# Layer 1 of a hybrid network: weight sums spread out, norms scaled two pairs ahead, biases split early, the second expert's sums fetched first

## The chip, the cores and the metric

The kernel runs on one core of a Trainium2 chip, in one launch. The metric is the device time of that core in microseconds (us), from a run's start to its end. Before the change, three runs took 3275.79, 3277.91 and 3279.31 us; the median is 3277.91 us. A core has five engines that matter here[...]: TensorE (PE in the profile; PEld is its loading of weights), VectorE (DVE), ScalarE (ACT), GpSimd (POOL) and SyncE (SP), which here only issues transfers.

## The reference, cut to what matters

All data is float32. Layer 0 is a convolution and attention block on images of 256 channels and 32 x 32 pixels, 8 of them; the change does not touch it. Layer 1 works on the same data as 8 sequences of 1024 tokens of width 256:

```python
t = _to_tokens(x)
t = t + _L1_attn_ref(_ln_t(t), WQ, WK, WV)          # causal softmax, one head of width 256
t = t + _L1_ffn_ref(_ln_t(t), Wr, br, W1, b1, ...)  # 8 experts, all of them, gated
# _ln_t:  (v - mean) / sqrt(var + 1e-5) over the last axis
# in _L1_ffn_ref:
feat = jnp.mean(x, axis=0)                          # over the 8 sequences
w = jax.nn.softmax(feat @ Wr + br, axis=-1)
h = relu(bn(x @ W1[e] + b1[e])); h = relu(bn(h @ W2[e] + b2[e]))
y = h @ Wo[e] + bo[e]                               # summed over e with weights w
```

Because the mean `feat` goes over all sequences, no expert's output can be weighted before all sequences have been through the attention.

## The kernel before, in words

**Order of the work.** The engines' proxies `pe`, `act`, `dve` and `pool` record every instruction at line 68 and keep them in the order in which the program issues them. That is why the profile gives line 68 for nearly everything; its groups are told apart by the names of the tiles. The order itself is made by generators. The function `together(main, side, ratio)` runs two of them: each `yield` of `main` adds its microseconds to a count, and `side` is advanced while its own count is below 0.85 of it. What is left of `side` at the end is issued in one go. The number in a `yield` is an estimate by the author, and only sets the order.

**Attention stage, batch by batch.** `causal(b)` is the main line of batch `b`: for each of eight rows of 128 queries, `scores` multiplies the row with all keys (tile `s`, in two halves `h`), takes the negated maximum on VectorE (`nm`) and the exponential on ScalarE (`pr`). `norm` then masks `pr`, sums it and takes the reciprocal on VectorE, and scales it on GpSimd. `turn`, some rows later, transposes `pr` through PSUM (`tp`) into `pT`, and `product` multiplies with the values (`po`) and adds to the tokens `t` on VectorE. The side line `beside(b)` prepares the next batch: `first_norm(b + 1)`, then `second_norm(b - 1)` (the norm ahead of the experts, `z2`, with `feat` summed on GpSimd), then `keys_values(b + 1)` (`pk`, `pv`). In the last batch the side line is `second_norm(6)`, `second_norm_half(7)` and `gate`, which makes the experts' weights `wT` for the first half of the tokens (tiles `lg`, `ge`, `pwT`).

**A norm (`layer_norm`).** Tokens are transposed in pairs of 128 (`tpt`, then a ScalarE copy to `zt`), VectorE takes statistics (`st`, `mv`), GpSimd the reciprocal root `r`. Four empty `yield 1.0` follow. Then `scaled(0)` scales the first pair on VectorE in place in `zt`; and for each pair, the next pair is scaled, the pair is transposed back (`tpz`) and copied by ScalarE. The transposes `tp`, `tpt` and `tpz` share one PSUM pool of two buffers (`ps_t`); `pk`, `pv` and `po` share another of two.

**Weight sums.** Layers of the experts are multiplied by Strassen-like schemes with seven products instead of eight (`by_seven`, `layer3`), for which `weight_sums` computes sums of blocks of the weights: for 20 weight matrices, four VectorE instructions each on 128 x 128 blocks, the third in place in the weights. Expert 0 keeps its sums in memory; for the others they are stored to DRAM (`sums_d`). `causal` calls `next(sums, None)` once per row, from batch 2 on.

**Between the stages.** The attention's pools are closed, and the experts' pool `hp` and three PSUM pools are opened; `hp` takes memory that the attention's tiles had. Then come the folding of the experts' batch norms, the splitting of the output biases `bo` into a rounded part and a rest (`bo4`, transposed through `pbo` to `boT`), and the transfers on SP: tokens of the first two pieces (`fetch(0)`, `fetch(1)`, tile `te`), the last batch's second half (`lastt`, `lastf`, in `last_norm`), and the 18 tiles of sums (`ws`), expert by expert.

**Expert stage.** It loops over 16 half batches and 8 experts. For each piece, layer 1 (`pa`), layer 2 of the piece two before (`pm`) and layer 3 of the piece four before (`q`, in four PSUM banks) are interleaved in four steps; `last_norm` advances beside the first pieces.

## Time and profile before

| | us |
|---|---|
| median of three runs | 3277.91 |
| the profiled execution: its time | 3277.43 |
| its span, first to last instruction | 3275.3 |
| TensorE busy | 3047.3 |
| VectorE busy | 2417.4 |
| ScalarE busy | 1438.2 |
| TensorE's wait for the scaling `zt`, 1415 to 2030 us | 39.9 |

Layer 0 takes the span's first 1400 us or so, the attention of layer 1 goes to about 2036 us, and the experts fill the rest, where TensorE is busy all the time (400.00 of 400 us between 2200 and 2600). A line of the order of time reads: start, duration, engine, line, operation, output and inputs, shape, count, and in brackets how long the engine sat idle before it and whose end released it. A line of the waits reads: who waited, for whom, us in total, how often, the longest. The mean granted clock of TensorE was 0.977 of full speed.

### The profile page before, as it was taken

Reading aid. Unit: us, or ns where it says so; the run is one execution under the profiler, and the core shown is the slowest. Engines: PE = TensorE matmul, PEld = TensorE weight load, DVE = VectorE, ACT = ScalarE, POOL = GpSimd, SP = SyncE. Lnnn points to the kernel's source line nnn. Section 1 sums busy time; section 2 is a strip of 40 time slices with the busy share of each in tenths; the row PEclk is TensorE's granted clock in tenths of the full one; section 3 lists DMA queues with packets and bytes.
Section 4 is the critical chain, followed back from the end, with each engine's and each line's share of the span. In section 5 each row is a group of like instructions: output and inputs, shape, how many; then the busy total and the mean of one; then the engine's idle time right before and its main releaser. Section 6 shows DMA issues by size and latency. Waiting matters only on the chain.

```text
span 3275.3 us, 43158 instructions
## 1 busy us (share of the span) xinstructions
PE 3047.3 (93%) x17218; PEld 2050.7 (63%) x17218; DVE 2417.4 (74%) x3796; ACT 1438.2 (44%) x2227; POOL 327.9 (10%) x472
## 2 busy tenths in 40 slices
PE   7997999999999997779999998899999999999999
PEld 4554555555555554346556665678787777787787
DVE  5388888888888886735555444688888878888887
ACT  4554555555555553223333322444444444444443
POOL 2110212111111100011222111000000000000000
PEclk9998999999999999889999999999999999999999
DMA  3202020202020200031111101200000100000000
GB/s 111 53 1 52 27 52 27 53 27 52 27 52 27 52 14 20 4 136 44 50 61 51 39 26 72 75 20 20 20 20 20 33 20 20 20 20 26 20 7 13
DMA packets 49831, 121.45 MB, mean 37 GB/s; under 512 B 7302, under 2 KB 20054, under 8 KB 45782
## 3 DMA queue, kind: packets, MB, share of 16 engines
q1 hardware_dynamic: 49622, 118.61, 11.6%
q8 instruction: 137, 2.24, 0.3%
q14 instruction: 72, 0.59, 0.1%
HBM read 48.20 MB, written 37.88 MB: 26 GB/s over the span
## 4 chain that ended last, share of the span: by engine, by line
PE 48%; DVE 6%; ACT 1%; issue 1%; POOL 1%; DMA 0%; SPq 0%; ACTq 0%; POOLq 0%; DVEq 0%
PE pm L68 13%; PE pa L68 12%; PE q L68 12%; PE s L68 4%; PE po L68 3%; PE pv L68 2%; PE pk L68 2%; DVE nm L68 1%; DVE pr L68 1%; DVE zt L68 1%; DVE st L68 1%; ACT pr L68 1%; PE tp L68 1%; PE tpz L68 1%; PE tpt L68 1%
## 5 line engine op out<-in xcount | busy, mean ns | idle before, releaser
L68 ACT ACTIVATE h<-h,bn_o,bn_s 128x512 f32<-128x512 f32 x384 | 308.7, 813 | 627.7 <-DVE h L68 627.6
L68 DVE SCALAR_TENSOR_TENSOR x<-hpad,vec,x 128x1024 f32<-128x1024 f32 x248 | 320.4, 1297 | 32.1 <-ACT x L68 25.9
L68 DVE SCALAR_TENSOR_TENSOR conv<-hpad,vec,conv 128x1024 f32<-128x1024 f32 x256 | 331.5, 1301 | 14.3 <-ACT conv L68 8.4
L68 PE MATMUL pm<-h,w 128*128 128x512 f32 (+1 forms) x768 | 321.5, 528 | 0.0
L68 ACT ACTIVATE pT<-s 128x1024 f32<-128x1024 f32 x256 | 261.5, 1024 | 128.1 <-PE s L68 127.0
L68 PE MATMUL po<-pT,vT 128*32 128x256 f32 x4096 | 276.7, 388 | 12.0 <-ACT pT L68 11.3
L68 PE MATMUL ph<-xn,piw 128*128 128x512 f32 x512 | 250.8, 615 | 22.7 <-ACT conv L68 14.2
L68 PE MATMUL s<-kk,z 128*128 128x512 f32 x512 | 242.0, 600 | 0.6 <-DVE pr L68 0.6
L68 PE MATMUL s<-qst,kst 128*128 128x256 f32 x1024 | 216.5, 334 | 0.0
L68 PEld LDWEIGHTS s<-qst,kst 128*128 128x128 f32 x1024 | 146.5, 191 | 88.5 <-issue 82.2
L68 PEld LDWEIGHTS pm<-h,w 128*128 128x128 f32 x768 | 146.9, 191 | 76.6 <-issue 62.6
L68 DVE TENSOR_TENSOR h<-pa,first 128x512 f32<-128x512 f32 x128 | 88.3, 689 | 136.0 <-PE pa L68 134.3
L68 ACT ACTIVATE hpad<-ph,pi_o 128x512 f32<-128x512 f32 x126 | 87.0, 690 | 228.5 <-PE ph L68 228.4
L68 DVE TENSOR_TENSOR h<-h,wb 128x1024 f32<-128x1024 f32 x128 | 156.2, 1221 | 41.0 <-ACT h L68 41.0
L68 DVE SCALAR_TENSOR_TENSOR o<-vpad,pe_w,o 128x1024 f32<-128x1024 f32 x128 | 163.6, 1283 | 17.4 <-ACT o L68 14.7
L68 DVE TENSOR_TENSOR h<-h,first 128x256 f32<-128x256 f32 x384 | 163.2, 425 | 13.2
L68 PEld LDWEIGHTS ph<-xn,piw 128*128 128x128 f32 x512 | 88.9, 190 | 132.1 <-issue 89.1
L68 PE MATMUL pz<-pow__117,hid 128*128 128x256 f32 x512 | 129.2, 408 | 44.4 <-DVE hid L68 44.4
L68 PEld LDWEIGHTS po<-pT,vT 128*32 128x32 f32 x4096 | 107.5, 109 | 97.1 <-ACT pT L68 15.2
L68 PE MATMUL sums<-pT,ones 128*32 128x256 f32 x2048 | 158.7, 382 | 0.0
L68 PE MATMUL pa<-tz,ws 128*128 128x256 f32 x512 | 155.0, 385 | 3.8 <-DMA ws<-sums_d 3.8
L68 PE MATMUL q<-t,ws 128*128 128x256 f32 x512 | 152.8, 380 | 0.8 <-DVE t L68 0.8
(279 smaller groups left out, 5870.6 us busy)
## 6 DMA issues: line engine op xcount, KB each, us to landing
td<-t SPq DMA_DIRECT2D x8, 1024.0 KB, 3.8
t<-td SPq DMA_DIRECT2D x8, 1024.0 KB, 4.8
te<-ud SPq DMA_DIRECT2D x16, 512.0 KB, 4.0
out_dram<-te SPq DMA_DIRECT2D x16, 512.0 KB, 2.8
ze<-zd SPq DMA_DIRECT2D x15, 512.0 KB, 3.9
t<-in_x_dram SPq DMA_DIRECT2D x7, 1024.0 KB, 6.3
qst<-hi SPq DMA_DIRECT2D x56, 128.0 KB, 2.3
qst<-lo SPq DMA_DIRECT2D x56, 128.0 KB, 2.3
```

Source lines behind the costliest of these rows:

```text
L68: return self._tc.keep_in_program_order(method(*args, **kwargs))
```

## The change

Five edits, all in layer 1. `weight_sums` yields after each of its instructions, and it is called from batch 1 on, twice a row: once after the row as before, and once in `scores` after the first half of the products. In `layer_norm` there are six empty steps instead of four, and two pairs are scaled ahead instead of one. The output biases are split at the start of batch 4, in a pool that lives through both stages. After the attention, the first transfers are the sums of expert 1, then `lastt` and `lastf`, the sums of expert 2, `fetch(0)`, the other sums, and `fetch(1)` last. What is computed is the same.

```diff
@@ weight_sums
                 dve.tensor_add(s_[:, 0, :], a21, a22)
+                yield
                 dve.tensor_sub(s_[:, 1, :], s_[:, 0, :], a11)
+                yield
                 dve.tensor_sub(a21, a11, a21)
+                yield
                 dve.tensor_sub(s_[:, 2, :], a12, s_[:, 1, :])
@@ layer_norm
-            for _ in range(4):
+            for _ in range(6):
                 yield 1.0
...
             scaled(0)
+            if n > 2:
+                scaled(2)
             yield 0.5
             for i0 in range(0, n, 2):
-                if i0 + 2 < n:
-                    scaled(i0 + 2)
+                if i0 + 4 < n:
+                    scaled(i0 + 4)
@@ causal
-                if b >= 2:
+                if b >= 1:
                     next(sums, None)
@@ scores
                     pe.matmul(s[:, hs], z[b][:, k, q0:width], kk_of[b][:, k, hs], start=(k == 0), stop=(k == KC - 1))
+                if h == 0 and b >= 1:
+                    next(sums, None)
                 yield 1.7
@@ the loop over batches; the same lines are taken out after the stage, where they used hp and ps_b
             if b == 4:
+                boT = wm.tile([4 * NE, KC, P], F32R, name="boT")
+                bo_g = cols("bo").rearrange("p (e g) -> p g e", g=KC).unsqueeze(2).to_broadcast([P, KC, 2, NE])
+                bo4 = wm.tile([P, KC, 4, NE], F32R, name="bo4")
+                dve.tensor_copy(bo4[:, :, 0:2, :], bo_g)
+                dve.tensor_sub(bo4[:, :, 2:4, :], bo_g, bo4[:, :, 0:2, :].bitcast(F32))
+                pb = ps_m.tile([4 * NE, KC, P], F32, tag="mm", name="pbo")
+                for g in range(KC):
+                    pe.transpose(pb[:, g, :], bo4[:, g].bitcast(F32).rearrange("p a e -> p (a e)"), ident)
+                dve.tensor_copy(boT, pb)
@@ ahead of the expert loop
+        def fetch_sums(e):
+            for l in (0, 1, 2) if seven(e) else (0, 2):
+                sums_of[e][l] = hp.tile([P, 3, P], F32, tag=f"ws{e}_{l}", name=f"ws{e}_{l}", bufs=1)
+                nc.sync.dma_start(sums_of[e][l], sums_d[e, l])
+
         zs[halves[0]] = z0
-        fetch(0)
-        fetch(1)
+        fetch_sums(1)
         between = last_norm()
         next(between)
+        fetch_sums(2)
+        fetch(0)
+        for e in range(3, NE):
+            fetch_sums(e)
+        fetch(1)
         tz[halves[0]] = tz0
-        for e in range(1, NE):
-            for l in (0, 1, 2) if seven(e) else (0, 2):
-                sums_of[e][l] = hp.tile([P, 3, P], F32, tag=f"ws{e}_{l}", name=f"ws{e}_{l}", bufs=1)
-                nc.sync.dma_start(sums_of[e][l], sums_d[e, l])
```

More of the change, by code (lines that the diff above doesn't have):

```diff
@@ L1587, in conv_attn_hybrid_kernel @@
         s2, o2 = bn_fold("g2", "be2", "m2", "v2", eps_moe, "bn2", extra="b2")
-        boT = hp.tile([4 * NE, KC, P], F32R, name="boT", bufs=1)
-        bo_g = cols("bo").rearrange("p (e g) -> p g e", g=KC).unsqueeze(2).to_broadcast([P, KC, 2, NE])
-        bo4 = hp.tile([P, KC, 4, NE], F32R, name="bo4", bufs=1)
-        dve.tensor_copy(bo4[:, :, 0:2, :], bo_g)
-        dve.tensor_sub(bo4[:, :, 2:4, :], bo_g, bo4[:, :, 0:2, :].bitcast(F32))
-        pb = ps_b.tile([4 * NE, KC, P], F32, tag="pm", name="pbo")
-        for g in range(KC):
-            pe.transpose(pb[:, g, :], bo4[:, g].bitcast(F32).rearrange("p a e -> p (a e)"), ident)
-        dve.tensor_copy(boT, pb)
         def sums_tile(name):
@@ L1804, in last_norm @@
             )
-        zs[halves[0]] = z0
-        fetch(0)
-        fetch(1)
-        between = last_norm()
-        next(between)
-        tz[halves[0]] = tz0
-        for e in range(1, NE):
+        def fetch_sums(e):
             for l in (0, 1, 2) if seven(e) else (0, 2):
@@ L1815, in conv_attn_hybrid_kernel @@
                 nc.sync.dma_start(sums_of[e][l], sums_d[e, l])
+        zs[halves[0]] = z0
+        fetch_sums(1)
+        between = last_norm()
+        next(between)
+        fetch_sums(2)
[3 more added lines that the diff above has]
+        fetch(1)
+        tz[halves[0]] = tz0
         LAG2, LAG3 = 2, 4
```

## The prediction

> **What bounds the kernel now.** I read the profiled execution's first part (busy shares), then TensorE's waits in the attention stage of layer 1 (1440 to 2035 us), then the order of time at those waits and at the hand-over to the expert stage (2035 to 2055 us).

> ```profile
> span 3275.3 us, 43158 instructions
> PE 3047.3 (93%) x17218; PEld 2050.7 (63%) x17218; DVE 2417.4 (74%) x3796; ACT 1438.2 (44%) x2227; POOL 327.9 (10%) x472
> ```

> TensorE is busy 93% of the span, so a gain is an idle stretch of TensorE that goes. The change touches only layer 1. TensorE's waits there, 1415 to 2030 us (engine, waited for, us in total, times, longest):

> ```profile
> PE tpz L68 <- DVE zt L68: 39.9, 32, 6.2
> PE tp L68 <- ACT pT L68: 4.3, 8, 0.6
> PE po L68 <- ACT pT L68: 2.3, 1, 2.3
> ```

> The transposes of the scaled norm, tpz, wait for VectorE's scaling, zt; 6.2 us of the 39.9 lie in the lone first norm at 1422, where nothing overlaps. About 34 us sit in the eight interleaved batches. Batch 6, whose sums are long done, in order of time, at its two norms:

> ```profile
> 1890.77 2.07 DVE L68 TENSOR_SCALAR zt<-zt,mv,r 128x256 f32<-128x256 f32 x6 [1.06 <-POOL r L68]
> 1891.38 0.67 PE L68 MATMUL tpz<-ident,zt 128*128 128x128 f32 x4 [0.83 <-DVE zt L68]
> ...
> 1921.21 0.16 DVE L68 RECIPROCAL rs<-rs 128x1 f32<-128x1 f32 x1
> 1921.29 2.50 DVE L68 TENSOR_SCALAR zt<-zt,mv,r 128x256 f32<-128x256 f32 x6
> 1921.84 0.41 PE L68 MATMUL tpz<-ident,zt 128*128 128x128 f32 x2 [0.68 <-DVE zt L68]
> ...
> 1928.09 0.41 PE L68 MATMUL tpz<-ident,zt 128*128 128x128 f32 x2 [1.54 <-DVE zt L68]
> ```

> zt runs the moment VectorE has finished the softmax row ahead of it (max nm, exp on ScalarE, mask and sum pr, reciprocal): VectorE is late by latency, not by load. Batch 2 has a whole group of weight sums in front of zt:

> ```profile
> 1616.20 0.80 DVE L68 TENSOR_TENSOR wo<-wo 128x128 f32<-128x128 f32 x1
> 1616.93 0.28 DVE L68 TENSOR_TENSOR ws<-wo,ws 128x128 f32<-128x128 f32 x1
> 1617.68 1.94 PE L68 MATMUL tpz<-ident,zt 128*128 128x128 f32 x8 [3.15 <-DVE zt L68]
> ```

> There the two norm stalls of this half are 3.15 and 2.10 us, against 0.68+0.31+1.54+0.41 = 2.9 without sums (batch 6): sums cost 2.3 us. The period from one first norm's tpz to the next says the same: 74.6 us (1510.12 to 1584.76), but 77.6 with sums (1584.76 to 1662.35). The hand-over:

> ```profile
> 2037.26 0.51 SPq L1566 DMA_DIRECT2D ud<-t  x1
> 2040.61 0.18 DVE L68 CAST bo<-vec 128x32 fp32r<-128x32 f32 x1 [3.37 <-DMA ud<-t]
> 2041.11 0.58 PE L68 MATMUL pbo<-ident,bo 128*32 128x128 f32 x2 [5.19 <-DVE bo L68]
> 2041.77 0.60 SPq L1762 DMA_DIRECT2D lastt<-ud  x1
> 2043.56 0.58 ACT L68 COPY first<-pa 128x512 f32<-128x512 f32 x1 [15.26 <-PE pa L68]
> 2050.43 0.81 PE L68 MATMUL pa<-tz,ws 128*128 128x256 f32 x2 [3.83 <-DMA ws<-sums_d]
> ```

> Two gaps: bo4 lies in the new pool, whose memory is free only when the last store ud<-t has landed; and expert 1's sums queue behind four 512 KB transfers.

> [...]pbo holds up pa, which needs nothing of it. [...]w<-w takes 0.28 us alone, 0.80 beside GpSimd's scaling at 1616. [...]after the 5.2 us gap the first pair of pa takes 0.86 us instead of 0.43.

> **Part 1, norms: scaled two pairs ahead, two more empty steps.** No arithmetic is added; the order changes. As built, the first norm's part becomes: tp (7), all of s1, tp (8), tpz0, half s2, tpz1, tpz2, half s2, tpz3, po. On VectorE: four zt, nm1, pr1, two zt, two zt. Walked with batch 6's durations (a half s is 1.72 us, four transposes 0.44, zt about 0.35 to 0.42 each): tp7 at 1887.90, s1 done 1892.1, tp8 done 1893.0. zt is ready long before (1891.4), so that wait goes. But tpz needs a transpose buffer of PSUM (two in all), and tp8 holds both. ScalarE empties them behind exp1, and exp1 needs nm1: s1 done and seen 1892.3, nm1 to 1893.5, exp1 0.4, copy 0.58: 1894.55. TensorE waits 1.6 us there, in place of 0.83+0.24+0.59; behind the waiting tpz stand s2 and po, and nm2 and the next exp wait for s2. Then 0.44+1.72+0.88+1.72+0.44: po starts at 1899.75; it started at 1900.49. Gain 0.7.

> The second norm's part becomes: tp3, s5 whole, tp4, half s6, tpz0, tpz1, half s6, tpz2, half po, tpz3, pk; on VectorE pr4, nm5, pr5, four zt, four zt. From tp3 = 0 (1917.23): TensorE reaches tpz0 at 0.33+3.44+0.44+1.72 = 5.93. s5 is ready at 3.97, nm5 to 5.2, exp5, pr5 (0.93 from exp to mask, 1.6 to the reciprocal) to 7.8, first zt 0.55: 8.35. A wait of 2.4, the chain now being one row later, but only one, since all of zt follows at once. pk then starts at 14.0 with half of po (1.52) already done; before, 13.68 without. Gain 1.2.

> **Part 2, sums one instruction at a time.** The same 80 instructions, two calls per row from batch 1 on, 16 a batch: done at the end of batch 5. They leave batches 2, 3 and the first half of 4 as clumps (worth 2.3 in a second half, 0.24 in a first, where the wait was 1.07 instead of 0.83). But in batches 1 to 5 a pair now stands ahead of nm5: 0.29 plus 0.28 to 0.80, so 0.6 to 1.1 on that chain, and another 0.56 before nm4, which the earlier bn_stats (0.66) cover. In the first half the pair hides in the wait for GpSimd's r (1.06). So a second half with sums gains 1.2-1.1 = 0.1. The 18 stores of sums wait on SP's queue for their fourth instruction, and with them the loads of t behind; those are wanted a batch (75 us) later.

> Batch by batch: 0: 1.5 (its 1.79 and 0.61 waits and the slow spread of eight tpz, less a 1.3 wait for the exp ahead of a buffer); 1 and 5: 0.8 each; 2 and 3: 0.94+2.4 = 3.3 each; 4: 0.94+1.1 = 2.0 (its second half now stalls 1.67+0.31+1.54+0.41 = 3.9, 1.0 above batch 6's); 6: 1.9; 7: its second norm 1.2. Sum 14.8.

> **The end of batch 7 loses.** The two extra steps push tpz1 of the last half norm to between the halves of the last po, directly ahead of lg. lg needs feat: copy 0.2+0.58, addition 1.22, hops: 2.15 us idle, where the same addition ran at 2020.41 beside tp. lg's 4.5 us and the softmax (3.0 us, under half po of 4.06) stay; two tp waits (0.38, 0.44) go into the earlier part. From end of the former po to pwT 18.2 against 16.9, and both tpt now before the second half of s7 push nm7 by 0.6: loss 1.9.

> **Part 3, biases split in batch 4.** Two VectorE instructions (0.18+0.19), two transposes, a 0.41 copy. VectorE is done with its last row some 2 us before TensorE ends pv (batch 5: 1875.9 against 1878.0), so only the transposes count: 0.5 lost there.

> **Part 4, the hand-over.** U = end of the last po (2035.3). The addition to t no longer stands behind the cast of wT: store issued at U+0.95, landing 3.0 later as before, seen at U+4.2. TensorE starts pa at once, but has two PSUM buffers; the third tile waits for the copy to first, whose memory is in the same pool: U+4.25. From that copy to expert 0's end it took 2.55 (2043.56 to 2046.11), plus pw 0.49: expert 1 at U+7.3. Its sums, first on the queue at U+4.2, take 2.6 us (the median of the 36 transfers of ws from issue to landing): U+6.8, hidden. Before: 2050.43 = U+15.1. Gain 7.8, less 0.4 for ScalarE's queue of expert 0 not yet drained. What is moved back: lastt, now behind 0.6 MB, is needed at U+12.2; 2.3 MB took 9.8 us before, an estimate of 0.29 MB/us after 2 us; it lands at U+10. Expert 2's sums, behind 1.6 MB: U+12.5, needed at U+16. te is needed 15 us later still. fetch(1) goes behind all sums and is wanted only after eight experts.

> **Sum.** 14.8-1.9-0.5+7.4 = 19.8. The profiled execution took 3277.4 (span 3275.3), 0.5 under the median of the runs: 3277.4-19.8 = 3257.6, with the median 3258.1; forecast 3258. The unknown waits: each of 15 norm parts could be 1 us worse (the PSUM buffer is late) or lose its wait altogether, the hand-over could give 4 (sums late) to 9[...].

> **Rivals.** (a) Stalls only move: the wait for zt becomes an equal wait for the exp ahead of a PSUM buffer, in all batches; for it, my walk already finds 1.6 and 2.4 us left; against it, the clumps of sums are gone. Only the hand-over less 0.5 remains: 3277.4-6.9 = 3270.5. (b) The scaling is truly ahead and nearly all of 34 us goes: 3277.4-34-7 = 3236; against it, four zt still follow pr5. (c) Slower: tp8, put as a block ahead of tpz, makes TensorE wait for nm, exp and two copies at each of 15 norm parts. At 1.6 us it still gains; it decides from 19.8/15 = 1.3 us more in each, and shows as slower from 1.8, which needs VectorE to start nm1 after 1894; then 3285. (d) That the change does nothing: excluded, the built order differs.

> **Chances.** Forecast 0.62 (own range 3247 to 3267), (a) 0.17, (b) 0.09, (c) 0.09, something else near no change 0.03. The measurement tells 0.2% (6.6 us) from nothing. (a) straddles that bound: faster 0.83, same 0.08, slower 0.09. Range 3240 to 3272.

> **What would show it.** tpz waiting for zt: down from 39.9 to about 25, of it none at first norms; new waits of tpz for ScalarE's pT copies, about 1.6 us each in batches 1 to 6. No zt wait above 3.2 beside the sums. lg waiting some 2 us for feat. The second expert's pa within 8 us of the last po, no wait for ws above 1. Wrong if: the waits on pT exceed 3 us, lastt or ws of expert 2 shows as a TensorE wait, or expert 1 starts beyond U+10.

## The result, and the profile after

The changed kernel takes 3267.27 us (median of six runs, 3266.08 to 3267.92), the kernel before 3278.61 in the runs beside it (3273.93 to 3281.05). The ratio is 0.9964 with a 95% interval from 0.9954 to 0.9974: 11.3 us faster, where 19.8 were forecast. The time lies just past the slow end of the forecast's own range (3247 to 3267) and inside the wide one (3240 to 3272). The profiled execution has a span of 3266.0 us, 9.3 below that of before.

From here on, "before" and "after" are the two kernels' profiled executions. The first part of the page of after, the busy shares:

```profile
span 3266.0 us, 43167 instructions
PE 3049.6 (93%) x17218; PEld 2053.9 (63%) x17218; DVE 2418.1 (74%) x3796; ACT 1440.3 (44%) x2227; POOL 327.9 (10%) x472
```

TensorE does the same 17218 instructions but is busy 2.3 us longer, in a span that is 9.3 us shorter. So its idle time shrank by 11.6 us, and something made the work itself 2.3 us slower. TensorE's waits of after in the attention of layer 1, 1415 to 2030 us (who, for whom, us in total, times, longest):

```profile
PE tpz L68 <- DVE zt L68: 26.9, 15, 6.5
PE tpz L68 <- ACT pT L68: 9.6, 7, 1.5
PE po L68 <- ACT pT L68: 4.9, 1, 4.9
PE lg L68 <- DVE feat L68: 1.9, 1, 1.9
```

The wait for `zt` fell from 39.9 to 26.9 us, in 15 waits instead of 32; the new wait for ScalarE's `pT` copies, 1.5 us each, and that of `lg` are where the prediction put them. `po`'s wait of 4.9 us was 2.3 before. TensorE in order of time, at the second norm beside batch 5 and the one beside batch 6 (start, duration, instruction, wait in brackets):

```profile
1841.39 0.41 PE L68 MATMUL tpz<-ident,zt 128*128 128x128 f32 x2 [2.52 <-DVE zt L68]
1842.22 1.08 PE L68 MATMUL tpz<-ident,zt 128*128 128x128 f32 x6 [0.42 <-DVE zt L68]
1843.13 3.27 PE L68 MATMUL s<-kk,z 128*128 128x512 f32 x4
...
1915.88 0.41 PE L68 MATMUL tpz<-ident,zt 128*128 128x128 f32 x2 [2.27 <-DVE zt L68]
1916.71 1.08 PE L68 MATMUL tpz<-ident,zt 128*128 128x128 f32 x6 [0.42 <-DVE zt L68]
1917.62 1.88 PE L68 MATMUL s<-kk,z 128*128 128x512 f32 x4
```

The same four `s` take 3.27 us in batch 5 and 1.88 in batch 6. That is TensorE's clock: the profile records the rate that TensorE is granted, and here it is either 1.00 or 0.50 of full speed. Reading it in stretches of 0.2 us, the spells of half rate in batches 1 to 5 begin at 1543.12, 1618.21, 1693.30, 1768.39 and 1843.49: 75.09 us apart. Each of the five lasts 3.41 us, and 75.09 is 22 times 3.413. From 1500 us on, all spells of this profile begin on one grid of 3.413 us and last one or two of its steps; in the other profiles too, each with its own offset. A step below is one step of this grid. On it, the same stretches of after (length, busy us of PE, PEld, DVE, ACT and POOL with counts, granted clock, DMA share, GB/s):

```profile
1836.66:1840.08 3.42, 2.21 (x9) 0.90 (x7) 2.36 (x6) 1.38 (x2) 0.88 (x1) 1.00 0.00 0
1840.08:1843.49 3.41, 1.68 (x9) 1.07 (x10) 3.34 (x12) 0.74 (x2) 0.91 (x1) 1.00 0.00 0
1843.49:1846.90 3.41, 3.41 (x8) 1.61 (x7) 1.47 (x5) 0.43 (x1) 0.00 (x0) 0.50 0.16 58
...
1911.75:1915.16 3.41, 1.86 (x6) 0.55 (x4) 2.31 (x5) 1.38 (x2) 0.27 (x1) 1.00 0.00 0
1915.16:1918.57 3.41, 2.27 (x11) 1.35 (x12) 3.38 (x10) 1.17 (x2) 0.91 (x1) 1.00 0.00 0
```

In batch 5, one step of the grid holds 1.73 us of idle time (3.41 - 1.68), and the next step runs at half rate. In batch 6 the wait (2.27 us) falls across a border, 1.55 and 1.14 us, and nothing follows. A step at half rate costs TensorE half its length if it has work all through; half of 3.41 us is 1.7, an estimate from these lengths. Between 1500 and 2097 us the profile of before has 9 steps at half rate and that of after has 15: six more, 10.2 us. The gain missing from the forecast, in the spans, is 19.8 - 9.3 = 10.5.

The hand-over of after, in order of time (SPq: SP issues a transfer):

```profile
2032.70 0.59 ACT L68 COPY first<-pa 128x512 f32<-128x512 f32 x1 [9.13 <-DMA ud<-t]
2032.73 1.28 SPq L1814 DMA_DIRECT2D ws<-sums_d  x3
2033.34 0.70 PE L68 MATMUL pa<-z,ws 128*128 128x256 f32 x2 [2.42 <-ACT first L68]
...
2041.65 0.60 PE L68 MATMUL tpt<-ident,lastt 128*128 128x128 f32 x4
```

`pbo` and its 5.2 us are gone, no `ws` is waited for, `lastt` is there in time. Expert 1 starts 7.1 us after `pwT` (2028.59 to 2035.69), where it took 15.1.

Where the 9.3 us of the spans lie (in us), by landmarks that both profiles have:

| stretch | before | after | gain | predicted |
|---|---|---|---|---|
| start to layer 1's first `tpt` | 1411.96 | 1413.72 | -1.8 | 0 |
| to the first `s` of batch 7 | 540.40 | 527.94 | 12.5 | 13.1 |
| batch 7, to `pwT` | 82.97 | 86.93 | -4.0 | -0.7 |
| to expert 1 | 15.10 | 7.10 | 8.0 | 7.4 |
| to the fourth expert (the `pw` ahead of its first `pa`) | 16.06 | 20.17 | -4.1 | 0 |
| to the end | 1208.81 | 1210.14 | -1.3 | 0 |

The first row is not the change: layer 0 is untouched. The last two are half rate, the matrix products being the same: six steps after (the first begins 1 us ahead of the row), two before.

### The profile page after: what moved, and what is told of

Same layout as the page of the kernel before. It is cut to its first block, busy times and chain, and to the rows that moved or that the text cites. A ratio compares the mean times of both kernels' runs of the same rounds, so it can differ in the third digit from the quotient of the medians.

```text
span 3266.0 us, 43167 instructions
## 1 busy us (share of the span) xinstructions
PE 3049.6 (93%) x17218; PEld 2053.9 (63%) x17218; DVE 2418.1 (74%) x3796; ACT 1440.3 (44%) x2227; POOL 327.9 (10%) x472
## 3 DMA queue, kind: packets, MB, share of 16 engines
q1 hardware_dynamic: 49622, 118.61, 11.6%
## 4 chain that ended last, share of the span: by engine, by line
PE 49%; DVE 5%; ACT 1%; issue 0%; DMA 0%; POOL 0%; ACTq 0%; POOLq 0%; DVEq 0%
PE pm L68 13%; PE pa L68 12%; PE q L68 12%; PE s L68 4%; PE po L68 4%; PE pv L68 2%; PE pk L68 2%; DVE nm L68 1%; PE tpz L68 1%; DVE pr L68 1%; DVE st L68 1%; ACT pr L68 1%; DVE h L68 1%; PE tpt L68 0%; PE tp L68 0%; DVE zt L68 0%
## 5 line engine op out<-in xcount | busy, mean ns | idle before, releaser
L68 ACT ACTIVATE h<-h,bn_o,bn_s 128x512 f32<-128x512 f32 x384 | 308.6, 813 | 627.7 <-DVE h L68 627.6
L68 DVE SCALAR_TENSOR_TENSOR x<-hpad,vec,x 128x1024 f32<-128x1024 f32 x248 | 320.4, 1297 | 32.1 <-ACT x L68 25.9
L68 DVE SCALAR_TENSOR_TENSOR conv<-hpad,vec,conv 128x1024 f32<-128x1024 f32 x256 | 331.6, 1301 | 14.4 <-ACT conv L68 8.4
L68 PE MATMUL pm<-h,w 128*128 128x512 f32 (+1 forms) x768 | 323.5, 531 | 0.0
L68 ACT ACTIVATE pT<-s 128x1024 f32<-128x1024 f32 x256 | 261.8, 1025 | 128.2 <-PE s L68 127.1
L68 PE MATMUL po<-pT,vT 128*32 128x256 f32 x4096 | 277.6, 389 | 11.0 <-ACT pT L68 10.3
L68 PE MATMUL ph<-xn,piw 128*128 128x512 f32 x512 | 250.8, 615 | 22.8 <-ACT conv L68 14.2
L68 PE MATMUL s<-kk,z 128*128 128x512 f32 x512 | 244.6, 607 | 0.7 <-DVE pr L68 0.6
L68 PE MATMUL s<-qst,kst 128*128 128x256 f32 x1024 | 216.7, 334 | 0.0
L68 PEld LDWEIGHTS s<-qst,kst 128*128 128x128 f32 x1024 | 146.8, 191 | 88.8 <-issue 82.5
L68 PEld LDWEIGHTS pm<-h,w 128*128 128x128 f32 x768 | 147.8, 193 | 77.4 <-issue 63.4
L68 DVE TENSOR_TENSOR h<-pa,first 128x512 f32<-128x512 f32 x128 | 88.3, 690 | 137.2 <-PE pa L68 132.3
L68 ACT ACTIVATE hpad<-ph,pi_o 128x512 f32<-128x512 f32 x126 | 87.1, 691 | 228.3 <-PE ph L68 228.3
L68 DVE TENSOR_TENSOR h<-h,wb 128x1024 f32<-128x1024 f32 x128 | 156.3, 1221 | 41.1 <-ACT h L68 41.1
L68 DVE SCALAR_TENSOR_TENSOR o<-vpad,pe_w,o 128x1024 f32<-128x1024 f32 x128 | 163.6, 1284 | 17.4 <-ACT o L68 14.7
L68 DVE TENSOR_TENSOR h<-h,first 128x256 f32<-128x256 f32 x384 | 163.2, 425 | 13.2
L68 PEld LDWEIGHTS ph<-xn,piw 128*128 128x128 f32 x512 | 88.8, 190 | 132.2 <-issue 89.2
L68 PE MATMUL pz<-pow__117,hid 128*128 128x256 f32 x512 | 129.1, 408 | 44.4 <-DVE hid L68 44.4
L68 PEld LDWEIGHTS po<-pT,vT 128*32 128x32 f32 x4096 | 107.6, 110 | 96.5 <-ACT pT L68 14.0
L68 PE MATMUL sums<-pT,ones 128*32 128x256 f32 x2048 | 159.0, 382 | 0.0
L68 PE MATMUL pa<-tz,ws 128*128 128x256 f32 x512 | 156.0, 387 | 0.0
L68 PE MATMUL q<-t,ws 128*128 128x256 f32 x512 | 152.7, 380 | 0.8 <-DVE t L68 0.8
```

The source lines that it names most:

```text
L68: return self._tc.keep_in_program_order(method(*args, **kwargs))
```

## The experiments

Theory: the change does what the prediction walked through, but the idle time that it leaves lies in longer pieces, which bring TensorE to half rate, and in batch 7 something makes the last row late. Rivals: the edits of the norm or of the sums themselves cost more than they save; the transfers slow TensorE at the hand-over; the waits only move. All ratios are to the kernel before, with 95% intervals; the last column counts steps at half rate from 1500 to 2097 us in each profile.

| kernel | median us | ratio | half-rate steps |
|---|---|---|---|
| before | 3278.61 | 1 | 9 |
| after | 3267.27 | 0.9964 (0.9954 to 0.9974) | 15 |
| norms only | 3280.93 | 1.0005 (0.9997 to 1.0014) | 19 |
| sums only | 3276.93 | 0.9994 (0.9986 to 1.0002) | 13 |
| hand-over only | 3267.45 | 0.9974 (0.9966 to 0.9981) | 7 |
| after, `feat` late | 3260.54 | 0.9947 (0.9934 to 0.9961) | 12 |
| after, 14 transposes | 3256.08 | 0.9925 (0.9911 to 0.9938) | 7 |
| after, hand-over filled | 3259.73 | 0.9941 (0.9927 to 0.9954) | 11 |
| after, seven steps | 3259.51 | 0.9938 (0.9925 to 0.9952) | 11 |
| seven steps, `feat` late, half norm as before | 3259.23 | 0.9936 (0.9922 to 0.9949) | 13 |
| after, 4 transposes | 3265.85 | 0.9961 (0.9947 to 0.9974) | 16 |
| all mended | 3249.43 | 0.9908 (0.9893 to 0.9923) | 4 |
| all mended, seven steps | 3250.58 | 0.9915 (0.9901 to 0.9928) | 5 |
| all mended, seven steps in the last | 3246.50 | 0.9902 (0.9885 to 0.9918) | 4 |

**Norms only.** Before, with these edits:

```diff
-            for _ in range(4):
+            for _ in range(6):
...
             scaled(0)
+            if n > 2:
+                scaled(2)
...
-                if i0 + 2 < n:
-                    scaled(i0 + 2)
+                if i0 + 4 < n:
+                    scaled(i0 + 4)
```

> Before plus the edits of the norm alone (two pairs ahead, six empty steps). Theory (the steps work as walked; half-rate spells of TensorE after the 2.5 us waits and a late last row give part of it back): the batches gain 0.4 to 1.3 us each, 6 in all, the end of the last batch loses 4, so 0 to 4 us faster than before, and in the profile a wait of tpz for zt of about 2.5 us in each second norm with a half-rate spell behind it. Rival (no clock effect, as predicted): the norms' own share of the sum, about 1.5 + 6 x 1.9 - 1.9 = 11 us faster. Rival (the longer wait costs more than the two it replaces): slower by over 3 us.

Measured: no difference, 1.0005; at best 1 us faster, at worst 4.6 slower. The prediction's 11 us are excluded; the theory's 0 to 4 holds only near its 0. The waits of this profile, 1415 to 2030 us, are those of after:

```profile
PE tpz L68 <- DVE zt L68: 28.4, 15, 6.4
PE tpz L68 <- ACT pT L68: 9.7, 7, 1.5
PE po L68 <- ACT pT L68: 4.8, 1, 4.8
```

In its batch 1, without sums, a period (first norm's `tpz` to the next) has 4.21 us idle instead of 4.97 and lasts 74.21 us instead of 74.64. But the profile has 19 steps at half rate, ten more than before: the edit that was to bring most of the gain brings nothing by itself, as what it saves in waits goes into the clock, and into the end of batch 7, where `po` waits 4.8 us as in after.

**Sums only.** Before, with the three new `yield`s, `b >= 1`, and the second call in `scores`.

> Before plus the sums one at a time, twice a row from batch 1. Theory (a pair costs only 0.25 us in a second half, the clumps cost 2.3 in two batches and 0.24 in three): 2 x 2.3 + 0.7 - 5 x 0.25 = about 4 us faster. Prediction's size of the pair (1.1): -0.2 to 0.2, no change. Rival (pairs in five batches are worse than clumps in three): slower by 1 to 3 us.

Measured: 0.9994, from 4.6 us faster to 0.7 slower; this can't tell the theory's 4 us from nothing, but excludes the last rival. In the profile the attention's idle time falls from 50.76 to 47.66 us, while the half-rate steps rise from 9 to 13.

**Hand-over only.** Before, with the biases split in batch 4 and the transfers in the new order; norms and sums as before.

> Before plus the early bias split and the new order of transfers, with norms and sums as before. Theory (the start 8 us earlier is real, the half-rate spell of 20 us behind it gives 4 back): 3 to 4 us faster; in the profile expert 1 starts within 8 us of the last product, and TensorE's clock is below 0.75 in the 20 us after. Prediction: 7 us faster. Rival (the spell belongs to the last batch's changed order, not to the hand-over): 7 us faster with the clock near 0.9 as before.

Measured: 0.9974, that is 8.5 us faster (6.2 to 11.1). My expectation of 3 to 4 was wrong, and the prediction's 6.9 lies in the interval. From `pwT` to the fourth expert it takes 24.54 us (before 31.16, after 27.27): 6.6 of the 10.7 us between the two spans. Another 4.7 us lie in layer 1 ahead of `pwT`, where only the bias split differs, 3.1 of them in batch 7 with one half-rate step less; they are not the hand-over's. In the last 16 us of this stretch the clock is at 0.99: the wait for `first` is even longer here (3.4 us), but one step of half rate follows, not four. So the half rate behind the hand-over is no fixed price of an early start: the steps behind hold at most 1.36 us of idle time here, where after has one with 2.05. In before itself, 31.16 us was a good draw: norms only and sums only issue the same instructions there and took 34.02 and 33.89. The single runs of this kernel spread over 14 us (3264.38 to 3278.52), more than any other.

**`feat` late.** In batch 7 of after, GpSimd's addition to `feat` (VectorE and GpSimd in order of time):

```profile
1991.11 4.54 POOL L68 TENSOR_TENSOR feat<-feat,z 128x2048 f32<-128x2048 f32 x1 [5.90 <-ACT z L68]
1992.57 3.23 DVE L68 TENSOR_TENSOR pr<-pr,lower 128x128 f32<-128x128 f32 x1
1999.36 1.19 DVE L68 TENSOR_REDUCE nm<-s 128x1 f32<-128x1024 f32 x1
...
2002.29 7.49 PE L68 MATMUL po<-pT,v 128*128 128x256 f32 x24 [4.85 <-ACT pT L68]
```

The mask of row 6 takes 3.23 us and ends at 1995.80, just behind GpSimd (1995.65); of the 64 masks the median takes 0.29, and in before, where none meets this addition, the longest took 0.33. `t<-t,po` ran beside the same addition in its usual 0.69 us; why the mask was slowed and this was not, no run shows. In each of the other five batches that have this addition it also meets a mask, which takes 1.50 us instead of 0.29 and ends with it; no wait of TensorE follows there. In batch 7, behind the mask stand the statistics and row 7's maximum, exponential and copies, for which `po` waits. The experiment moves the addition and the store of `feat` behind it:

```diff
@@ layer_norm(..., meanwhile=None), behind the root r
+            if meanwhile:
+                meanwhile()
@@ second_norm
-            else:
+            elif b < B - 2:
                 pool.tensor_add(feat, feat, z2)
+            else:
+                z2_6.append(z2)
@@ second_norm_half: meanwhile is
+            def feat_6():
+                pool.tensor_add(feat, feat, z2_6[0])
+                nc.sync.dma_start(feat_d, feat[:, :, HALF:])
```

> The changed kernel, with GpSimd's addition of batch 6 to feat (4.5 us) moved from the end of the second norm of batch 6 to behind the root of the last half norm. Theory (in the changed kernel this addition lies across VectorE's mask of row 6, which then takes 3.23 us instead of 0.29, and the last maximum, exponential and copies are late by it, so the last product waits 4.85 instead of 2.34 us): the mask is short again, the wait falls to about 2 us, and the kernel is 2 to 3 us faster than the changed one, some 14 us faster than before. Rival (the last row is late because two transposes were moved ahead of it): the wait stays above 4 us and nothing changes.

Measured: 0.9947, some 6 us better than after by the ratios (0 to 11 with both intervals taken together), so the times alone hardly show it. In this profile:

```profile
1992.48 0.28 DVE L68 TENSOR_TENSOR pr<-pr,lower 128x128 f32<-128x128 f32 x1
...
2000.13 4.52 POOL L68 TENSOR_TENSOR feat<-feat,z 128x2048 f32<-128x2048 f32 x1
...
2000.32 6.71 PE L68 MATMUL po<-pT,v 128*128 128x256 f32 x24 [2.97 <-ACT pT L68]
```

The mask is short and `po`'s wait 1.9 us shorter, as the theory had it; the rival's two transposes, which still stand ahead, can be the reason for at most the 0.6 us that the wait is above that of before. `pwT` comes 2.9 us earlier. The rest of the 7.2 us between the two spans is half rate that fell otherwise: 2.9 between `pwT` and the fourth expert, where nothing was edited, and 1.5 later.

**14 transposes of the identity.** These give TensorE something to do while it waits; they leave the wait's end where it was, and the real transposes overwrite them.

```diff
                 tp = ps_t.tile([P, KC, 2, P], F32, tag="tp", name="tpz")
+                if i0 == 0 and second:
+                    for _ in range(14):
+                        pe.transpose(tp[:, 0, 0, :], ident, ident)
```

> The changed kernel, with 14 transposes of the identity (about 1.5 us at full rate) in front of the first tpz of each second norm of eight tiles, into the same PSUM tile, which the real transposes then overwrite; all else, the wait's end too, as in the changed kernel. Theory (the 2.5 us wait puts TensorE to half rate for about 3.4 us, 1.7 us lost in each of batches 1 to 5): the wait falls to about 1 us, s behind it takes 1.88 instead of 3.27 us, and the kernel is 6 to 9 us faster than the changed one (about 3260). Rival (half-rate spells fall where they do whatever TensorE does just before, or the load is what brings them): no faster than the changed one, or slower by what of the 1.5 us doesn't fit in the waits.

Measured: 0.9925, 12.8 us better than after by the ratios (about 7 to 18 with both intervals taken together). TensorE in this profile, the same place as above:

```profile
1837.27 1.69 PE L68 MATMUL tpz<-ident 128*128 128x128 f32 x14
1839.87 0.44 PE L68 MATMUL tpz<-ident,zt 128*128 128x128 f32 x2 [0.91 <-DVE zt L68]
1840.79 1.08 PE L68 MATMUL tpz<-ident,zt 128*128 128x128 f32 x6 [0.48 <-DVE zt L68]
1841.71 1.88 PE L68 MATMUL s<-kk,z 128*128 128x512 f32 x4
```

`s` is back at 1.88 us. The periods of batches 1 to 5, 74.28, 74.66, 74.97, 74.74 and 74.74 us in after, are 73.06, 73.06, 73.28, 73.06 and 73.06 here: 7.9 in all, about 1.6 each. This shows that the clock, and no change of order, took the gain of the norms back. What goes beyond some 8 us lies, in the profile, mostly at the hand-over, which drew 24.34 us here instead of 27.27.

**4 transposes.**

> The changed kernel with 4 transposes of the identity (0.45 us) instead of 14 in front of the first tpz of each second norm. The wait was 2.52 us in batches 1 to 5, with a half-rate spell in each, and 2.27 us in batch 6, without one; it falls to about 2.1. Theory with a sharp limit on the idle time, between 2.27 and 2.52 us: no spell in batches 1 to 5, 8 us faster than the changed kernel, as with 14. Rival (it matters where the idle time falls, or how busy TensorE is over a longer stretch): spells in some of the five batches, 1.7 us each, 0 to 6 us faster.

Measured: 0.9961, no better than after. The wait is shorter than the 2.27 us that batch 6 bore without harm, and the spell is there all the same:

```profile
1836.14 0.60 PE L68 MATMUL tpz<-ident 128*128 128x128 f32 x4
1838.73 0.44 PE L68 MATMUL tpz<-ident,zt 128*128 128x128 f32 x2 [2.00 <-DVE zt L68]
1839.65 1.08 PE L68 MATMUL tpz<-ident,zt 128*128 128x128 f32 x6 [0.48 <-DVE zt L68]
1840.57 3.29 PE L68 MATMUL s<-kk,z 128*128 128x512 f32 x4
```

So the length of the wait is not what decides, and the theory of a sharp limit was wrong. The steps ahead of these five spells still hold 1.72 to 2.47 us of idle time; the step ahead of the wait in batch 6 of after held 1.55.

**Hand-over filled.** A helper makes transposes into the PSUM that `q` uses only later: 18 ahead of the third `pa` of expert 0, 16 ahead of the second `pg`.

```diff
+        def filler(n):
+            w_ = ps_q.tile([P, 2, QC], F32, tag="q0", name="warm")
+            for _ in range(n):
+                pe.transpose(w_[:, 0, :P], ident, ident)
```

> The changed kernel, with 18 transposes of the identity between the second and third pa of the first expert and 16 between the two pg, into the still unused PSUM of q. Theory (half rate at the hand-over follows the 2.4 and 2.0 us waits): the stretch from pwT to the pw of the fourth expert falls from 27.3 to about 24, clock above 0.9 there, 3 us faster than the changed kernel. Rival (the spell comes from the 300 GB/s of transfers in that stretch): the clock stays near 0.7, no gain.

Measured: 0.9941, some 7 us better than after (2 to 13), of which 4.7 lie in this stretch of the profile. `pwT` to the fourth expert takes 22.59 us with the clock at 1.00 and the same transfers as in after (258 to 385 GB/s in the steps from 2031.99 to 2049.05; in after 261 to 389 from 2034.63 to 2051.70), so they don't bring the half rate. TensorE's lines:

```profile
2028.14 2.13 PE L68 MATMUL warm<-ident 128*128 128x128 f32 x18
2030.72 0.70 PE L68 MATMUL pa<-z,ws 128*128 128x256 f32 x2 [0.46 <-ACT first L68]
...
2042.44 1.88 PE L68 MATMUL pm<-h,w 128*128 128x512 f32 x4
```

The first four `pm` take 1.88 us; in after they took 3.62. Kernels with the new hand-over but without the transposes took 24.3 to 27.4 us here, as the waits fell on the grid; the four with them took 22.59, 23.61, 24.14 and 27.24. So they bring up to 5 us and don't always suffice: in the slowest of the four, all mended with seven steps, the store of `t` landed later, and `first` was waited for 3.36 us in spite of them.

**Seven steps, and two combinations.** With seven empty steps in the norms of eight tiles; then with `feat` late and the half norm of the last batch as before the change.

```diff
-            for _ in range(6):
+            for _ in range(7 if n > 4 else 6):
```

> The changed kernel with seven empty steps instead of six in the norms of eight tiles (six in the half norm): half a row of s (1.72 us) more stands ahead of the first tpz, in both norms. Theory (the waits of 1.5 and 2.5 us are TensorE being early by so much, and the spell follows the longer one): the first goes, the second falls to about 0.8, no half-rate spell behind it; 1.5 + 1.7 + 1.7 us in each of batches 1 to 5, 10 to 25 us faster than the changed kernel. Rival (the waits are set by the chain of the softmax rows and only move to the next product): within 4 us of the changed kernel.

> Seven empty steps as in the run before, with GpSimd's addition to feat late, and the half norm of the last batch as it was before the change (four steps, one pair ahead). Theory (the three causes are separate and add): 6 us from the addition and some 2 us from lg, which no longer waits for feat, on top of what seven steps bring; 3233 to 3250. Rival (the last row, not feat, sets the end of the last batch): no more than 2 us better than seven steps alone.

Measured: 0.9938 and 0.9936. The first is some 8 us better than after (3 to 14), between the two expectations, and not for the theory's reason. TensorE beside batch 5, seven steps:

```profile
1838.63 3.67 PE L68 MATMUL s<-kk,z 128*128 128x512 f32 x8 [0.47 <-DVE pr L68]
1844.56 1.62 PE L68 MATMUL tpz<-ident,zt 128*128 128x128 f32 x8 [2.25 <-DVE zt L68]
1845.97 3.05 PE L68 MATMUL po<-pT,v 128*128 128x256 f32 x8
```

The wait moved behind the whole next row, since VectorE now takes that row's maximum and mask ahead of `zt`; the half rate moved with it (`po` 3.05 us, 1.68 at full rate). The periods are 74.97, 75.00, 75.22, 75.01 and 74.43 us, in all no shorter than after (374.6 against 373.4): the rival was right for the batches. The gain is in the last one. From batch 6's first `tpz` to `pwT` it takes 136.7 us (after 143.1): the rows fall otherwise, the `feat` addition misses the mask, and `po` waits 2.3 us again. The second kernel takes 132.9 there, with no wait of `lg` left, but loses as much to half rate at the hand-over (27.37 instead of 24.53) and behind it. The theory's 3233 to 3250 was wrong; the rival's number came out, though its reason did not, since the last batch did get 3.8 us shorter.

**All mended.** 16 transposes in the second norms, the filled hand-over, `feat` late, and the half norm with four steps and one pair ahead; the same with seven steps and 12 transposes; and with seven steps, and 4 transposes, in the last batch's second norm alone.

> The changed kernel with all that helped: 16 transposes of the identity in the wait of each second norm, 18 and 16 at the hand-over, GpSimd's addition to feat late, and the last half norm with four steps and one pair ahead. Theory (the causes are separate): 8.4 from the batches, 6 from the last batch, 3 to 5 from the hand-over, against the changed kernel: 3243 to 3252, faster than every kernel so far. Rival (they share one cause): 3254 to 3258, no better than with the first transposes alone.

> The same with seven empty steps and 12 transposes. In seven steps' own profile the wait of the second norm moved behind the whole next row and stayed at 2.25 us with a spell behind it in batches 1 to 5 (period 74.97 us). Theory: the transposes take the spell away here too, 1.7 us in each of five batches; 3242 to 3250, within 3 us of the run before. Rival (where the wait stands matters): over 3 us slower than the run before.

> The kernel with all that helped (six steps), but seven steps and only 4 transposes in the one second norm that runs beside the last batch. From batch 6 on, the two kernels above took 137.1 us with six steps and 131.8 with seven, up to pwT; batches 0 to 5 took 3.5 less with six. Theory (the order of the last batch's rows sets its end, and each batch is separate): both gains together, 4 to 6 us faster than with six steps throughout, 3243 to 3246. Rival (the 5.3 us were half-rate windows that fell differently): within 2 us of it, 3248 to 3251.

Measured: 0.9908, 0.9915 and 0.9902. All three beat both kernels; the last is the best, 32 us faster than before (27 to 38; about 3 times the gain of the change), and its profile has 4 half-rate steps. The first keeps to its 3243 to 3252, against 3254 to 3258 for one shared cause, so the causes are separate. It is 18 us better than after by the ratios; the three single edits (13, 6 and 7) come to 26, each give or take 5, and in their profiles part of each gain is half rate that fell well where nothing was edited. The first two can't be told apart, and the third's 3 us over the first lie within the intervals and between its two expectations, which stay undecided; in the profile, batch 6's first `tpz` to `pwT` fell from 137.1 to 134.0 us, less than the 131.8 that was hoped for. The span and the waits of the last kernel (its page, and 1415 to 2030 us):

```profile
span 3244.3 us, 43428 instructions
...
PE tpz L68 <- DVE zt L68: 14.1, 16, 6.3
PE tpz L68 <- ACT pT L68: 9.6, 7, 1.5
```

## Why the prediction was right and wrong, by its steps

- **First norms (Part 1): right.** TensorE waits 1.49 us for `pT` (predicted 1.6), and from tp7 to `po` it takes 11.97 us in batch 6, where it took 12.59: gain 0.62, predicted 0.7.
- **Second norms (Part 1): the order right, the price incomplete.** The wait is 2.27 us in batch 6 (predicted 2.4), and `pk` starts 14.20 us after tp3 with half of `po` done (predicted 14.0): gain 1.0, predicted 1.2. What was left out is the half-rate step behind the one long wait, 1.7 us in each of batches 1 to 5. The prediction has a pair of `pa` at half the pace behind a gap of 5.2 us (0.86 us instead of 0.43) and priced no such loss behind its own waits. Another line that it shows had the sign: behind the wait of 3.15 us in batch 2 of before, in a step at half rate that begins at 1617.34, eight `tpz` take 1.94 us, where eight take 1.04 at full rate. It put all of that batch's 3.0 us to the sums; 2.2 of them are idle time (7.15 against 4.97 us), and 0.8 are longer busy time. With the transposes in place, the clean period of batch 1 is 73.06 us against 74.64: 1.6 gained, 1.8 with the pair of sums below, which is the predicted 1.9.
- **Sums (Part 2): the pair was priced four times too high.** The wait at `tpz` is 2.52 us with a pair and 2.27 without: 0.25, not up to 1.1. In five batches that gives about 4 us back. It hid the two half-rate steps that batches 1 to 5 have more than before (3.4 us); so the row "to the first `s` of batch 7", 12.5 us for 13.1, is right by two errors that cancel.
- **End of batch 7: the order right, a delay mis-sized.** The wait of `lg` came as walked (1.94 us, predicted 2.15). But "push nm7 by 0.6" was 2.5 us by `po`'s wait (4.85 instead of 2.34), because GpSimd's addition to `feat` now lies across the mask of row 6. That VectorE can be slower beside GpSimd (0.80 us instead of 0.28) was priced for the sums, and not looked up for what the change moves. With one more half-rate step the batch lost 4.0 us instead of 0.7.
- **Biases (Part 3).** They are split in batch 4 as planned. Hand-over only has this edit without the norms and the sums: the period with the split takes 77.95 us there and 77.57 in before, while the other four of batches 1 to 5 agree within 0.03. The loss is 0.4, predicted 0.5.
- **Hand-over (Part 4): right, to its end.** Expert 1 starts 7.1 us after `pwT`, which begins at about U (predicted U+7.3), its sums and `lastt` are hidden, and alone it brings 8.5 us (6.2 to 11.1; predicted 6.9). One number was luck: the 2.6 us for a transfer of sums is a median over the stores of sums and the loads together; of before's 18 loads alone the median is 4.2. Now ahead of the queue, one of the first landed in 2.57. In after the stretches behind it then gave 5.4 us back to half rate, a term that the walk doesn't have.
- **The sum.** 19.8 was predicted and the spans show 9.3. The step of the prediction that failed is the clock: it took TensorE's rate as that of before, and six more steps at half rate, over batches, end and hand-over, are 10.2 of the 10.5 us between the two numbers. The match is partly luck: the 2.5 us of `feat` and 1.8 us of layer 0 are made up for by the cheaper sums.
- **Rivals.** (a), 3270.5, is nearer in number than the forecast, and not by its mechanism alone. TensorE's waits at `tpz` did fall by only 5 us in all (41.6 with those for `z` before, 36.5 with those for `pT` after), but a wait costs more than its bracket: a clean period has 4.97 us idle before and 4.43 after, but 1.1 us less busy time as well (69.67 in batch 1 of before; in batch 5 of after 70.31, of which 1.71 are half rate). With seven waits per period before and three after, that is an estimate of about 0.27 us for each wait beyond what its bracket shows; why, no run shows. (b) had no part. (c) is wrong as stated: the block of tp8 costs 1.49 us and gains. What held the change near the side of no gain is a mechanism that no rival named.

## What to carry to other kernels

Before joining several short waits of TensorE into one long one, count the clock: cut the span into the steps in which the granted clock changes (3.41 us here), and see how much idle time a step will hold. Here half rate followed each of the 73 full-rate steps with 2.0 us or more of it, and 18 of the 44 with 1.5 to 2.0; behind the joined wait it cost an estimated 1.7 us, half a step, on top of the wait's length. Transposes of a constant into a PSUM tile that is to be overwritten anyway filled the wait of 2.52 us at no cost that the periods show (about 1.6 us shorter each), with enough of them (14, in 1.69 us, were; 4, in 0.60 us, were not) and their end before the wait's. When work moves on GpSimd, look at which VectorE instructions it will now lie across, and what the profile has for these beside GpSimd (here a mask took 3.23 and 1.50 us instead of 0.29, `t<-t,po` its usual 0.69), above all in the last batch, where nothing absorbs the delay.

## What was not expected of the hardware

```profile
2004.30 0.61 PE L68 MATMUL lg<-wrs,feat 128*128 128x8 f32 x4
...
2003.39:2006.80 3.41, 3.41 (x24) 3.19 (x24) 0.38 (x2) 0.23 (x1) 0.00 (x0) 1.00 0.12 44
2006.80:2010.22 3.42, 3.42 (x10) 2.71 (x9) 0.97 (x5) 0.00 (x1) 0.00 (x0) 0.50 0.02 5
```

With the time of `lg` counted as idle, each of the 16 full-rate steps of before and after with 2.0 us or more is followed by half rate, and none of the 293 below 1.3. That a wait ahead of `lg` and `lg` itself add up is my reading of the profiles alone; no kernel here changes `lg`.

- The loop of after stayed on that grid. Its periods of 74.3 to 75.0 us are close to 22 steps (75.09), so the wait falls on nearly the same part of a step in five batches running: idle 2.52, 2.65, 2.21, 2.08, 1.73 us in the step ahead of the half rate, then 1.55 in batch 6, and no spell. That a period half a step longer or shorter would not be hit each time is an estimate from these numbers; it was not tried.
- Why a spell lasts two steps in some places, with TensorE busy throughout (2034.63 to 2041.46 in after), and one in others, stays open. The first steps of the six such pairs in before and after hold 1.79 us of idle time (one), or 1.87 and 2.99 us of `lg` (two), or 0.79 us of `pw` (three; 32x512 products with 32 rows); the twelve spells of one step hold at most 0.53 us of idle time, and neither of the two. Open too is the spread of 14 us over the single runs of the hand-over alone.
